# VectorE's order in the slots of an attention pipeline: statistics and division ahead of q, reciprocal behind v, output projection in the last block

## Chip, cores and metric

The kernel runs on one core of a Trainium2 chip. The metric is the device time of one execution in microseconds (us). The kernel before takes 1013.86 us, the median of three runs (1013.26 to 1014.37). All operands are float32.

## What is computed

Sixteen sequences of 256 tokens with 256 features go through three attentions and a feed-forward part. Each attention has 16 heads of 16 features.

```
layer 0 (cross):  q = rms(x) @ Wq ; k, v = rms(ctx) @ Wk, Wv
                  x = rms(x + softmax(q k' * scale) v @ Wo)
layer 1 (self):   h = ln(x) ; q, k, v from h ; rope(q, k) ; causal softmax
                  x = x + attention @ sa_wo
layer 2 (cross):  h = ln(x) ; q from h, k and v from ctx ; rope(q, k)
                  x = x + attention @ ca_wo
feed-forward:     x + gelu(ln(x) @ fc1) @ fc2
```

## The kernel before

There are 48 attentions, three for each sequence. `ORDER` (line 31) lists their layers in the order of work: "000001101102102...102112122222". The loop at line 698 has one slot for each of them. Slot i computes the scores and values of attention i in blocks, four for layers 0 and 2 and three for the causal layer 1, and between the blocks it does pieces of its neighbours. The order of all instructions is written out by hand[...].

A block n of slot i begins with `scores(n)` (lines 463 to 497): TensorE computes scores (L476), ScalarE takes the exponential (L487), and for the causal layer GpSimd cuts the upper triangle (L494). `values(n - 1)` follows: TensorE multiplies the block before with v (L515); the last values of attention i-1 are done in block 0 of slot i. When the values of a feature half are complete, ScalarE copies them out (L529). The sums of the softmax come with them as an extra row, and the SyncE queue carries them through DRAM into a compact tile `sums` (L530, L539), while eight transfers put the values into `oT` (L544).

The pieces for the neighbours are these. The names are methods of `Att`.

- `stats(i + 2)`: mean and variance, or mean squares, on VectorE (L246, L256, L257), then an inverse root on GpSimd (L238, L239).
- `norm(i + 2)`: VectorE applies it (`xn`, L263). `turn(i + 2)`: TensorE transposes `xn` (L274) and ScalarE copies it out as `hT` (L279). Layer 0 has neither, its input is loaded transposed.
- `q(i + 1)` and `k(i + 1)`: projections on TensorE (L294). For layers 1 and 2 ScalarE adds the bias (`a`, L402), VectorE rotates (L406 to L435) and writes `qm` (L428) or `kT` (L435). For layer 0 VectorE writes `qm` from PSUM (L421) and ScalarE copies k (L437).
- `v(i + 1)`: a projection (L307), taken out of PSUM into `va` by VectorE (L448 or L456).
- `invert(i - 1)`: VectorE's reciprocal of `sums` (L553, L554), a check sum on GpSimd (L555), and two transfers through DRAM into the tile `first` (L556, L560).
- `divide(i - 2)`: VectorE spreads `first` over the features (L566) and multiplies `oT` with it (L570).
- `project(i - 2)`: the output projection on TensorE (L307), and the residual on VectorE (L576 or L579). For layer 0 mean squares (L246) and an inverse root on GpSimd follow.
- `finish(i - 2)`: for layer 0 alone, VectorE's last scaling (L584).
- `send` and `receive` (i + 2): for layer 0 alone, a small transpose on VectorE (L368) and transfers that spread the inverse root of x as `rq`.

In slot i of the kernel before, block 0 has stats, q and divide; block 1 has k and norm; the block before the last has project and send; the last block has finish, v, turn, receive and invert. In a slot of layer 1 the block before the last is block 1.

Projections, transposes and output projections share a PSUM pool of three buffers (`psD`, line 158). `fold_bias` (L189) and `fold_v` (L219, L226) fold biases into weights once, in block 0 of slot 2; `fold_gain` (L230) scales the weights in slots 2 to 4. After slot 47 comes a short passage with the last output projections, and then the feed-forward part for eight pairs of sequences (L622, L636, L641, L651, L660).

Of the kernel before, what the change touches and what calls it, by code (L numbers as in the profile page):

```python
# [46 lines left out]
def xattn_kernel(  # L47
# [56 lines left out]
    def load(b):  # L104
        load_x(b)
        load_y(b)

    def load_w(t, aps, eng):
        at = 0
        for a in aps:  # L110
            m = a.shape[1]
            eng.dma_start(out=t[:, :, at : at + m], in_=a.rearrange("(k p) n -> p k n", p=P))
            at += m
# [65 lines left out]
    def fold_bias():  # L179

        ps = dense_ps()
        sets = (
            [(sa_sb, 0, V_B1), (sa_sb, D, V_B1), (ca_sb, 0, V_B2), (ca_sb, 0, V_B2)],
            [(fc1_sb, j * D, V_B3) for j in range(4)],
        )
        for n, items in enumerate(sets):
            for k in range(KC):
                for j, (w, at, vcol) in enumerate(items):
                    nc.tensor.matmul(  # L189
                        ps[32 * j : 32 * j + 32, n * D : (n + 1) * D],  # L190
                        lhsT=vec[:, vcol + k : vcol + k + 1].to_broadcast([P, 32]),
                        rhs=w[:, k, at : at + D],
                        start=(k == 0), stop=(k == KC - 1), skip_group_check=True,
                    )
        sb = work.tile([P, 2 * D], F32, tag="a", name="fold")
        nc.scalar.copy(sb, ps)
        hop = dram.tile([4, 2 * D], F32, tag="fold", name="fold_hop", bufs=1)
        nc.sync.dma_start(out=hop, in_=sb[0:P:32])
        cols = ctile([P, 4, 2, KC], "cols")
        nc.sync.dma_start(  # L200
            out=cols.rearrange("p j n t -> p (j n t)"),
            in_=hop.rearrange("j (m p) -> p (j m)", p=P),
        )
        return cols

    def fold_cols(cols):
        qk = vec[:, V_QK : V_QK + 8].rearrange("p (n t) -> p n t", t=KC)
        nc.vector.tensor_tensor(qk_bias[:, 0:3], cols[:, 0:3, 0], qk[:, 0:3], ALU.add)
        nc.vector.tensor_copy(qk_bias[:, 3], qk[:, 3])
        nc.vector.tensor_tensor(  # L210
            fb1.rearrange("p (j t) -> p j t", t=KC), cols[:, :, 1],
            vec[:, V_FC1B : V_FC1B + FF // P].rearrange("p (j t) -> p j t", t=KC), ALU.add,
        )

    def fold_v():
        ps = dense_ps()
        for k in range(KC):
            for j in range(0, P, 32):
                nc.tensor.matmul(  # L219
                    ps[j : j + 32, :D],  # L220
                    lhsT=vec[:, V_B1 + k : V_B1 + k + 1].to_broadcast([P, 32]),
                    rhs=sa_sb[:, k, 2 * D : 3 * D],
                    start=(k == 0), stop=(k == KC - 1), skip_group_check=True,
                )
        row = bias_sb[:, R_SAV : R_SAV + D]
        nc.vector.tensor_tensor(row, ps[:, :D], row, ALU.add)  # L226

    def fold_gain(w, cols, vcol):
        for k in range(KC):
            nc.vector.tensor_scalar(  # L230
                w[:, k, cols], w[:, k, cols], vec[:, vcol + k : vcol + k + 1], None, ALU.mult
            )
# [358 lines left out]
    def att(i):  # L591
        if 0 <= i < N_ATT:
            return atts.setdefault(i, Att(i))
        return None

    def do(i, *names):
        a = att(i)
        for name in names:
            if a is not None:
                getattr(a, name)()  # L600
# [73 lines left out]
    def check(good, ones):  # L674
        ps = dense_ps()
        nc.tensor.matmul(ps[:1, :1], lhsT=good, rhs=ones, start=True, stop=True)
        nc.vector.tensor_copy(rows_good, ps[:1, :1])
# [3 lines left out]
    with tc.manual_schedule():  # L681
        do(0, "stats_x")
        fold_gain(w0_sb, slice(0, D), V_GQ)
        fold_gain(w0_sb, slice(D, 2 * D), V_GC)
        do(0, "turn", "spread", "q", "k", "stats_y")
        fold_gain(w0_sb, slice(2 * D, 3 * D), V_GC)
        nc.vector.tensor_copy(mask01, mask_u8)
        for va in vas:
            nc.gpsimd.memset(va[:, :, :, HD:], 1.0)
        do(1, "stats", "turn")  # L690
        load(3)
        load_w(sa_sb, sa, nc.sync)

        kept = {}
        for j in range(N_ATT):
            slot = next(i for i in range(max(j - 1, 0), N_ATT + 1) if (ORDER + [0])[i] != 1)
            kept.setdefault(slot, []).append(j)
        for i in range(N_ATT):
            a, last = att(i), att(i - 1)
            ahead = att(i + 3)  # L700
            if i > 1 and ahead is not None and ahead.layer == 0:
                load(ahead.b)
            for n in range(len(a.blocks)):
                a.scores(n)
                if n > 0:
                    a.values(n - 1)
                elif last is not None:
                    last.values(-1)
                final = len(a.blocks) - 1
                if n == 0:  # L710
                    if i == 0:
                        a.v()
                        do(1, "spread")
                    do(i + 2, "stats")
                    do(i + 1, "q")
                    do(i - 2, "divide")
                elif n == 1:
                    do(i + 1, "k")
                    do(i + 2, "norm")
                    for j in kept.get(i, ()):  # L720
                        att(j).keep()
                if n == final - 1:
                    do(i - 2, "project")
                    do(i + 2, "send")
                if n == final:
                    do(i - 2, "finish")
                    do(i + 1, "v")
                    do(i + 2, "turn", "receive")
                    do(i - 1, "invert")
                if i == 0 and n == 0:  # L730
                    load(4)
                    nc.sync.dma_start(out=bias_sb, in_=rows.partition_broadcast(P))
                    nc.sync.dma_start(out=turn_sb, in_=turn)
                if i == 0 and n == 1:
                    load_w(ca_sb, ca, nc.sync)
                if i == 0 and n == 2:
                    load_w(fc1_sb, [fc1], nc.sync)
                if i == 1 and n == 0:
                    load_w(sao_sb, [sa_o], nc.sync)
                    load_w(cao_sb, [ca_o], nc.sync)  # L740
                if i == 1 and n == 2:
                    load_w(fc2_sb, [fc2], nc.sync)
                    nc.sync.dma_start(
                        out=rope_sb, in_=rope.rearrange("(c p) t d -> p c t d", p=P)
                    )
                if i == 2 and n == 0:
                    cols = fold_bias()
                    fold_v()
                if i == 2 and n == 3:
                    fold_gain(sa_sb, slice(0, 3 * D), V_G1)  # L750
                if i == 3 and n == 3:
                    fold_cols(cols)
                    fold_gain(ca_sb, slice(0, D), V_G2)
                if i == 4 and n == 3:
                    fold_gain(fc1_sb, slice(0, FF), V_G3)
                if i == N_ATT - 2 and n == 1:
                    mlps[0].norm()
                if i == N_ATT - 1 and n == 2:
                    mlps[0].turn()
                if i == N_ATT - 1 and n == 3:  # L760
                    mlps[1].norm()

        last = att(N_ATT - 1)
        last.values(-1)
        do(N_ATT - 2, "divide")
        mlps[0].up(0)
        mlps[0].up(1)
        do(N_ATT - 2, "project")
        last.invert()
        mlps[0].up(2)  # L770
        mlps[1].turn()
        mlps[0].up(3)
        last.divide()
        last.project()
        for g in range(B // 2):
            if g > 0:
                for n in range(4):
                    mlps[g].up(n)
            if 0 < g and g + 1 < B // 2:
                mlps[g + 1].norm()  # L780
                mlps[g + 1].turn()
            mlps[g].down(0)
            mlps[g].down(1)
            if g == 1:
                found = count()
            if g == 2:
                check(*found)
# [411 lines left out]
```

## Time and profile before

The profile's span is 1012.3 us. Busy times by engine:

| engine | busy us | share of the span |
|---|---|---|
| TensorE (matmul) | 969.3 | 96% |
| VectorE | 555.8 | 55% |
| ScalarE | 535.9 | 53% |
| GpSimd | 276.0 | 27% |

The slots run from 10.9 us to about 775.6 us, where the feed-forward part starts. In the stretch from 800 to 1012 us VectorE is busy for 38.06 of 212 us; between 200 and 600 us it is busy for 68 to 70 us of each 100.

How to read it: TensorE is busy nearly all the time, so the places where it idles say what the other engines cost. A high average share of another engine says little, since it is the order of work within a slot that decides whether TensorE finds its input ready. In a timeline a line has its start, the time that it took, the engine, the line of the code, the operation, output and input, the count, and in brackets the engine's idle time ahead of it with what ended that.

### The profile page before, as it was taken

What the parts mean: (1) busy time and instruction counts of PE and PEld (TensorE: products, weight loads), DVE (VectorE), ACT (ScalarE), POOL (GpSimd) and SP (SyncE); (2) the same over time, 40 slices, a digit from 0 to 9 for tenths busy, and PEclk for the clock granted to TensorE, in tenths of its full rate; (3) what the DMA queues carried; (4) which work ended last, traced back from release to release, by engine and by line L of the source; (5) the groups of instructions that cost most, each with busy time, mean ns of one, the idle gap of its engine ahead of it and who ended that gap; (6) DMA issues with size and microseconds to landing.
All of it is one profiled execution on the core that took longest, in us unless ns stands there. A gap on an engine that the chain in (4) does not pass through costs nothing.

```text
span 1012.3 us, 28536 instructions
## 1 busy us (share of the span) xinstructions
PE 969.3 (96%) x11798; PEld 509.5 (50%) x11798; DVE 555.8 (55%) x1300; ACT 535.9 (53%) x709; POOL 276.0 (27%) x494
## 2 busy tenths in 40 slices
PE   8999899999999999999999998898998999999997
PEld 3444444454444444454544444444443766666765
DVE  4358676767766667767767667766664112222200
ACT  4567375666666576766666665465665122221221
POOL 3213544241433333241423332332213011111100
PEclk9999999999999999999999999999999999999999
DMA  9512121221212121211212111010001000000000
GB/s 320 165 33 63 26 63 28 69 61 34 65 29 67 30 63 30 69 45 46 67 29 69 26 24 26 15 23 21 20 22 27 12 21 15 17 22 21 22 22 24
DMA packets 65826, 46.86 MB, mean 46 GB/s; under 512 B 25364, under 2 KB 64788, under 8 KB 65688
## 3 DMA queue, kind: packets, MB, share of 16 engines
q1 hardware_dynamic: 64456, 43.89, 16.0%
q8 instruction: 95, 1.56, 0.7%
q10 hardware_dynamic: 1232, 1.07, 0.3%
q14 instruction: 43, 0.35, 0.1%
HBM read 26.54 MB, written 5.79 MB: 32 GB/s over the span
## 4 chain that ended last, share of the span: by engine, by line
PE 67%; DVE 15%; DMA 9%; SPq 3%; POOL 2%; issue 2%; ACT 1%; DVEq 0%; ACTq 0%; POOLq 0%
PE d L307 16%; PE S L476 11%; PE S L651 11%; PE d L636 11%; PE A L515 9%; PE d L294 8%; DMA hop<-sums 3%; DVE oT L570 3%; DVE inv L566 3%; DMA sums<-hop 2%; DMA yT<-in_yt 2%; SPq L544 2%; DVE qm L428 2%; DMA oT<-av 1%; PE d L274 1%
## 5 line engine op out<-in xcount | busy, mean ns | idle before, releaser
L487 ACT ACTIVATE pt<-S 128x1024 f32<-128x1024 f32 x224 | 217.4, 1022 | 151.5 <-PE S L476 151.3
L476 PE MATMUL S<-qm,kT 32*128 32x512 f32 (+1 forms) x1536 | 205.0, 603 | 1.3 <-ACT kT L437 0.7
L515 PE MATMUL A<-pt,va 128*32 128x256 f32 (+1 forms) x3072 | 189.2, 367 | 1.4 <-DVE sums L554 1.0
L487 ACT ACTIVATE pt<-S,sy 128x1024 f32<-128x1024 f32 x128 | 135.7, 1112 | 52.0 <-PE S L476 50.5
L515 PEld LDWEIGHTS A<-pt,va 128*32 128x32 f32 x3072 | 80.1, 109 | 156.4 <-issue 88.9
L641 ACT ACTIVATE gT<-d,fb 128x512 f32<-128x512 f32 x64 | 43.9, 687 | 164.3 <-PE d L636 164.3
L651 PE MATMUL S<-fc,gT 128*128 128x256 f32 x512 | 111.9, 380 | 0.0
L636 PE MATMUL d<-hT,fc 128*128 128x512 f32 x256 | 111.9, 594 | 0.0
L555 POOL TENSOR_TENSOR seen<-seen,sums 128x64 f32<-128x64 f32 x48 | 16.5, 344 | 345.5 <-DVE sums L554 343.0
L494 POOL TENSOR_SCALAR_AFFINE_SELECT pt<-pt 128x512 f32<-128x512 f32 x128 | 91.3, 731 | 57.0 <-ACT pt L487 57.0
L651 PEld LDWEIGHTS S<-fc,gT 128*128 128x128 f32 x512 | 97.0, 191 | 13.4 <-issue 0.9
L660 DVE TENSOR_TENSOR res<-S,cur 128x512 f32<-128x512 f32 (+1 forms) x17 | 11.1, 660 | 160.0 <-PE S L651 160.0
L476 PEld LDWEIGHTS S<-qm,kT 32*128 32x128 f32 x1536 | 62.9, 185 | 69.1 <-issue 34.3
L636 PEld LDWEIGHTS d<-hT,fc 128*128 128x128 f32 x256 | 48.4, 190 | 57.6 <-issue 56.5
L402 ACT ACTIVATE a<-d,qk_bias 128x256 f32<-128x256 f32 x128 | 53.7, 470 | 34.9 <-PE d L294 30.2
L283 POOL TENSOR_TENSOR cur<-cur,bias 128x512 f32<-128x512 f32 x48 | 60.8, 1271 | 4.4 <-DVE xn L263 4.4
L294 PE MATMUL d<-hT,sa 128*32 128x256 f32 x1024 | 61.1, 379 | 0.0
L263 DVE TENSOR_SCALAR xn<-cur,bmv,r_ln 128x256 f32<-128x256 f32 x96 | 48.6, 547 | 18.1 <-POOL r_ln L239 18.1
L238 POOL TENSOR_SCALAR r_ln<-bmv 128x2 f32<-128x2 f32 x48 | 10.5, 218 | 175.2 <-DVE bmv L257 174.3
L529 ACT COPY av<-A 128x512 f32<-128x512 f32 x96 | 56.7, 591 | 1.2 <-PE A L515 1.2
L456 DVE TENSOR_TENSOR va<-d,bias 128x512 f32<-128x512 f32 x32 | 22.1, 690 | 59.7 <-PE d L307 59.7
L406 DVE LOAD_MASK_SELECT u<-a x64 | 0.9, 14 | 86.6 <-ACT a L402 86.6
(105 smaller groups left out, 1228.4 us busy)
## 6 DMA issues: line engine op xcount, KB each, us to landing
oT<-av SPq DMA_DIRECT2D x384, 32.0 KB
cur<-in_x SPq DMA_DIRECT2D x16, 256.0 KB
xT<-in_xt SPq DMA_DIRECT2D x16, 256.0 KB
yT<-in_yt SPq DMA_DIRECT2D x16, 256.0 KB
y<-in_y SPq DMA_DIRECT2D x16, 256.0 KB
out<-res SPq DMA_DIRECT2D x15, 256.0 KB
fc<-in_fc SPq DMA_DIRECT2D x2, 1024.0 KB
rq<-rq_hop SPq DMA_DIRECT2D x14, 128.0 KB
```

What stands on the lines that cost most here:

```text
L263: nc.vector.tensor_scalar(xn[:, c, :], src[:, c, :], mv[:, c, 0:1], r[:, c : c + 1], ALU.subtract, ALU.mult,)
L283: nc.gpsimd.tensor_tensor(t, t, bias_sb[:, row : row + D].unsqueeze(1).to_broadcast([P, NC, D]), ALU.add)
L294: nc.tensor.matmul(ps[j : j + 32, t * S : (t + 1) * S], lhsT=w[:, k, at + t * P + j : at + t * P + j + 32], rhs=src[:, k, :], start=(k == ...
L307: nc.tensor.matmul(ps[j : j + 32, c * D : (c + 1) * D], lhsT=src[:, k, c * P + j : c * P + j + 32], rhs=w[:, k, at : at + D], start=(k == ...
L402: nc.scalar.activation(a[:, t], ps[:, t], AF.Identity, bias=bias[:, t : t + 1])
L476: nc.tensor.matmul(ps[:, j, 2 * m * u : 2 * m * (u + 1)] .rearrange("p (i s) -> p i s", i=2), lhsT=self.kT[r, t, kc * P : (kc + 1) * P], r ...
L487: nc.scalar.activation(pt[:, :, :w], ps[:, :, :w], AF.Exp, scale=scale)
L494: nc.gpsimd.affine_select(out=diag, in_=diag, compare_op=ALU.is_ge, fill=0.0, base=0, pattern=[[0, 2], [0, 2], [1, P]], channel_multiplier=-1,
L515: nc.tensor.matmul(self.av[32 * r : 32 * r + 32, i, q0:S], lhsT=self.va[:, kc, 8 * t + 2 * r + i, :], rhs=pts[r // 2][:, r % 2, i * m : (i ...
L529: nc.scalar.copy(av, self.av)
L636: nc.tensor.matmul(ps, lhsT=fc1_sb[:, k, f * P : (f + 1) * P], rhs=self.hT[:, k].rearrange("p i s -> p (i s)"), start=(k == 0), stop=(k == ...
L651: nc.tensor.matmul(ps[:, c, :D], lhsT=self.gT[f // 2][:, f % 2, i, c * P : (c + 1) * P], rhs=fc2_sb[:, f, :], start=(f == 0), stop=(f == F ...
```

## The change

The change moves calls within a slot. It removes no work and adds none.

- `divide(i - 2)` goes ahead of `q(i + 1)` in block 0, behind `stats(i + 2)`.
- `finish`, until now in the last block for attention i-2, is done in block 0 of the slot after, ahead of `stats` there: `do(i - 3, "finish")`.
- `v(i + 1)` and, behind it, `invert(i - 1)` go from the last block into the block before the last.
- `project(i - 2)` goes from the block before the last into the last block.
- `fold_bias` and `fold_v` go from block 0 of slot 2 into block 3 of slot 1.

It is meant to give VectorE its work in the order in which other engines need it, and to give the output projection more time until its input must be ready.

```diff
                     if i == 0:
                         a.v()
                         do(1, "spread")
+                    do(i - 3, "finish")
                     do(i + 2, "stats")
+                    do(i - 2, "divide")
                     do(i + 1, "q")
-                    do(i - 2, "divide")
                 elif n == 1:
                     do(i + 1, "k")
                     do(i + 2, "norm")
                     for j in kept.get(i, ()):
                         att(j).keep()
                 if n == final - 1:
-                    do(i - 2, "project")
+                    do(i + 1, "v")
+                    do(i - 1, "invert")
                     do(i + 2, "send")
                 if n == final:
-                    do(i - 2, "finish")
-                    do(i + 1, "v")
+                    do(i - 2, "project")
                     do(i + 2, "turn", "receive")
-                    do(i - 1, "invert")
...
-                if i == 2 and n == 0:
+                if i == 1 and n == 3:
                     cols = fold_bias()
                     fold_v()
```

## The prediction

> **What bounds the kernel now.** I read the busy times first, then TensorE's waits, then the timeline of one slot with a long wait.
>
> ```profile
> PE 969.3 (96%) x11798; PEld 509.5 (50%) x11798; DVE 555.8 (55%) x1300; ACT 535.9 (53%) x709; POOL 276.0 (27%) x494
> ```
>
> TensorE (PE) sets the end; it idles for 1012.3 - 969.3 = 43.0 us. The view of waits for PE says on whom:
>
> ```profile
> PE d L307 <- DVE oT L570: 31.8, 37, 3.9
> PE A L515 <- DVE sums L554: 1.0, 1, 1.0
> PE S L476 <- ACT pt L487: 0.6, 3, 0.3
> ```
>
> Three quarters of it is the output projection waiting for the divided `oT`: 37 waits, the longest 3.9 us. The timeline of slot 39 (layer 1), first PE, then VectorE (DVE):
>
> ```profile
> 625.64 1.91 PE L294 MATMUL d<-hT,sa 128*32 128x256 f32 x32
> 631.21 3.22 PE L307 MATMUL d<-w0o,oT 128*32 128x256 f32 x32 [3.66 <-DVE oT L570]
> ```
>
> ```profile
> 624.70 0.74 DVE L406 STREAM_SHUFFLE u<-a 128x512 f32<-128x512 f32 x1
> ...
> 628.27 1.51 DVE L428 TENSOR_SCALAR qm<-a,vec 128x512 f32<-128x512 f32 x2
> 629.72 0.01 DVE L566 LOAD_MASK_SELECT inv<-first  x1
> 629.72 0.71 DVE L566 STREAM_SHUFFLE inv<-first 128x512 f32<-128x512 f32 x1
> 630.46 0.69 DVE L570 TENSOR_TENSOR oT<-oT,inv 128x512 f32<-128x512 f32 x1
> 631.08 0.01 DVE L406 LOAD_MASK_SELECT u<-a  x1
> ```
>
> The division costs 1.4 us and waits for nothing itself. It comes late because q's rotation stands ahead of it in VectorE's queue, 5.02 us from 624.70 to 629.72, and VectorE had idled 3.07 us before that for ScalarE's `a`. The projection behind the wait took 3.22 us instead of 1.91. The table by windows shows why:
>
> ```profile
> 104.00:124.00 20.00, 18.64 (x288) 9.47 (x292) 13.27 (x33) 7.92 (x10) 7.99 (x14) 0.91 0.10 22
> 204.00:224.00 20.00, 20.00 (x324) 10.29 (x320) 12.05 (x30) 12.10 (x16) 10.47 (x19) 1.00 0.12 28
> ```
>
> The last columns are granted clock, DMA share and GB/s. After the 3.91 us wait at 104 us the clock is 0.91 over 20 us: 9% of 20 is 1.8 us lost. The waits of 3.66, 3.70 and 3.66 us (slots 39, 40, 42) are followed by such a loss too; the one of 3.25 us (slot 8) isn't.
>
> [...] L426 takes 1.00 us and the L428 pair 1.51 us in slot 39, where GpSimd cuts triangles, but 0.69 and 0.88 us in slot 13.
>
> **Part by part.** Steps on PE, start to start in the timeline: scores 1.07, values 0.89 (causal: 0.46, or 1.33 for the last), a projection 1.84, transposes 0.59 us. On VectorE: division 1.4, q rotated 3.6 (5.0 beside triangles), k 2.7, norm 0.65, v 0.6, reciprocal 0.35 to 0.55, layer 0's residual with mean squares 1.6, 1.1 until GpSimd's root, finish 0.9 to 1.6, statistics 1.2 (layer 0: 2.0, to 2.6 contended). From the end of a reciprocal until `first` has come I find 3.6 us at best (785.59 to 789.18) and 6.3 at worst (112.36 to 118.62); I take 4, and 6.3 where `rq` travels behind it.
>
> *Project later, divide earlier.* In slot 39 the projection would start v + scores + values = 1.84 + 1.07 + 0.46 = 3.37 us later, and the division is 5.0 us earlier: 8.4 us against a longest wait of 3.9. I expect this wait to go everywhere.
>
> *Plain slots, 10 to 37.* Read start to start of a slot's first scores, they take 430.78 us (172.87 to 603.65): layer 0 mostly 16.65, layer 2 15.65, layer 1 13.29, three of them 14.69, 14.10 and 14.69. Even a wait shown as 0.24 us costs 0.42 (613.63 is 0.42 past 612.32 + 0.89). Without it: 10 x 16.23 + 9 x 15.23 + 9 x 13.29 = 419.0, a gain of **11.8**. Is a new wait added? Behind the divide, which now waits for `first`, stand q, k, norm, v and reciprocal; PE waits for norm at turn, and for k a slot later. For a layer 0 slot, from its start: residual and root until 2.3, finish 3.9, statistics 5.1, divide 6.6 (`first` in by 1.4 to 4), q 10.2, k 13.0, norm 13.7. Turn needs it at 15.6: hidden, 1.9 us to spare. A layer 2 slot has no turn, and k is done at 11, slot end 15.2. In a layer 1 slot q is 1.4 and k is ScalarE's: spare. Finish, statistics, v and reciprocal therefore cost nothing.
>
> *Crowded slots.* Where a three-block slot rotates q and k (5, 8, 39, 40, 42), VectorE has 12.4 to 18.2 us of work for some 13 us of PE. Chaining the durations above:
> - Slots 5 to 9 take 80.3 us now (92.56 to 172.87). Without any wait 69.5. But the statistics (2.6), divide and q of slot 5 put kT at 15.0 us, and slot 6 wants it at 12.8: 2.2 wait. I get 71.9, saving 8.4.
> - Slots 38 to 42 take 89.25 (603.65 to 692.90), 72.8 without waits. Finish, statistics, divide, q, k and norm of slot 40 end 2.4 us after turn wants them; slots 39 and 42 miss by 0.4 each. With smaller slips 76.35, saving 12.9.
> - GpSimd's check sum now waits for the late reciprocal with the last triangles queued behind it, and the values of the next slot wait for these: 0.5 (39), 0.5 (40), 0.2 (42), 1.2 (5), 0.8 (8). `rq` comes late for slot 6: 1.0. Together -4.2.
> Net **17.1**. None of these waits reaches 3.25 us, so no half clock.
>
> *Start.* In slot 1 blocks 2 and 3 have no PE work between them, so scores wait for ScalarE: values start at 40.02 instead of 38.59. Now v stands in block 2 and the fold (2.7 us, moved as it is) in block 3: **1.45**. Its weights were loaded by 32 us, when DMA falls to 20 GB/s, and it would run near 42: no wait. *Slots 4 and 43 to 46*: 0.42 each, **2.1**. *Passage after slot 47*: the 2.31 us wait goes (three steps later), the reciprocal for the next one comes a little late: **2.2**.
>
> Sum 11.8 + 17.1 + 1.45 + 2.1 + 2.2 = 34.7, so 1013.86 - 34.7 = **979**.
>
> **Rivals.**
> *A, everything is gained.* If VectorE's slips in the crowded slots stay hidden, slots 5 to 9 take 69.5 and 38 to 42 72.8: 1013.86 - (10.8 + 16.5 + 11.8 + 1.45 + 2.1 + 2.8) = 968. For it: VectorE idles 3 us for `a` before most rotations now, which the divide fills. Against it: its 18.2 us of work in slot 5.
> *B, the wait only changes place in the crowded slots.* Turn, scores or triangles wait as long as the projection did, with the half clock: the 17.1 is lost, 996. For it: VectorE busy for 14.9 and 14.0 us in slots 39 and 40. Against it: until now the idle 3 us lay ahead of q.
> *C, slower.* The divide's wait for `first` now holds back q, k and norm in every slot. If `first` comes over 3 us after VectorE, the 28 plain slots lose some 1.5 us each at turn: 979 + 42 = 1021. For it: VectorE waited 16.6 us in 10 waits for `first`, and some trips took 6 us. Against it: the reciprocal comes a block earlier, so by the chain above even 6.3 us is covered in a layer 0 slot.
>
> **How the numbers follow.** Forecast 0.62, A 0.12, B 0.2, C 0.06. Between forecast and B all mixtures are possible, since the landing of `first` (3.6 to 6.3) and the contended rotation (3.6 to 5.0) move the crowded slots by 2 us each, ten slots by 10 to 14. So I put the range from 970, short of A, to 993, short of B. Slower is C less a little: 0.04; same 0.02; faster 0.94.
>
> **What would show it.** PE's wait for `oT` near zero instead of 31.8 us; slots of 16.2, 15.2 and 13.3 us in the middle; the clock at 1.00 after 100 us; new PE waits for kT in slot 6 and for `xn` at turn of slots 39, 40, 42, and on GpSimd's triangles, 8 to 10 us in all. Wrong would be: VectorE waiting long for `first` with PE waiting behind it in plain slots (C), or half clock still in slots 39 to 42 (B).

## The result, and the profile after

The kernel after takes 977.68 us, the median of four runs (977.05 to 978.01); the kernel before took 1013.67 us beside it. The ratio is 0.9644, with an interval of 0.9627 to 0.966. The forecast was 979 us in a range of 970 to 993. The profile's span falls by 37.1 us, from 1012.3 to 975.2.

The busy times on the page of the kernel after:

```profile
PE 959.1 (98%) x11798; PEld 512.1 (53%) x11798; DVE 555.9 (57%) x1300; ACT 536.4 (55%) x709; POOL 278.7 (29%) x494
```

VectorE and ScalarE did the same work. TensorE idles for 975.2 - 959.1 = 16.1 us instead of 43.0, and it is busy for 10.2 us less with the same 11798 matmuls. Most of those 10.2 us is the clock: in the slots of the kernel before lie four stretches of half clock (granted clock 0.50; the first from 104.81 to 108.22 us), each 3.41 us long and so worth 1.7 us, and in those of the kernel after none (1.00 from 10 to 740 us).

The waits of TensorE in the kernel after (for whom, then us in total, times, the longest):

```profile
PE S L476 <- DVE kT L435: 2.5, 1, 2.5
...
PE d L307 <- ACT gT L641: 1.7, 1, 1.7
PE d L274 <- DVE xn L263: 1.6, 1, 1.6
...
PE d L274 <- ACT av L529: 0.5, 2, 0.3
```

No wait stands under `oT` any more. (The one under `gT` ends with `oT` all the same; the last experiment comes back to it.) What has taken the place of the 37 waits is few and short. TensorE's timeline shows where (start, us, line, operation, count, and in brackets the idle time ahead of it): at the start of slot 6, in slots 39 and 42 (39 is shown), at the end of slot 40 and in the passage after slot 47.

```profile
102.51 1.93 PE L307 MATMUL d<-w0o,oT 128*32 128x256 f32 x32
106.91 1.14 PE L476 MATMUL S<-qm,kT 32*128 32x512 f32 x8 [2.46 <-DVE kT L435]
...
610.64 1.93 PE L307 MATMUL d<-w0o,oT 128*32 128x256 f32 x32
612.82 0.67 PE L274 MATMUL d<-ident,xn 128*128 128x128 f32 x4 [0.25 <-ACT av L529]
...
629.04 0.67 PE L274 MATMUL d<-ident,xn 128*128 128x128 f32 x4 [1.61 <-DVE xn L263]
...
745.82 1.93 PE L307 MATMUL d<-cao,oT 128*32 128x256 f32 x32 [1.65 <-ACT gT L641]
```

The output projection of slot 39, which had waited 3.66 us and then run for 3.22, starts at once and takes 1.93. VectorE's timeline of the same slot shows the new order:

```profile
600.99 0.75 DVE L566 STREAM_SHUFFLE inv<-first 128x512 f32<-128x512 f32 x1
601.77 0.69 DVE L570 TENSOR_TENSOR oT<-oT,inv 128x512 f32<-128x512 f32 x1
604.56 0.01 DVE L406 LOAD_MASK_SELECT u<-a  x1 [2.10 <-ACT a L402]
...
612.27 0.73 DVE L263 TENSOR_SCALAR xn<-cur,bmv,r_ln 128x256 f32<-128x256 f32 x2
```

The division is done at 602.46, 8.2 us before the projection asks for it, and the idle time for ScalarE's `a`, 3.07 us before, is 2.10. The last line is where the price is paid: `xn` comes at the very end, and the transposes wait for it.

The table by windows, in the first of the two stretches that the prediction showed (the last three columns are granted clock, DMA share and GB/s):

```profile
104.00:124.00 20.00, 17.12 (x275) 8.88 (x268) 15.06 (x36) 9.04 (x12) 10.31 (x20) 1.00 0.12 27
```

In this run the clock stays at 1.00 there, although TensorE still idles for 2.9 of the 20 us after 104 us.

Read in the timeline from the first scores of one slot to those of another, the 37.1 us lie here:

| stretch | before, us | after, us | gain | predicted |
|---|---|---|---|---|
| to the start of slot 5 | 92.56 | 91.17 | 1.4 | 1.9 |
| slots 5 to 9 | 80.31 | 74.17 | 6.1 | 5.4 |
| slots 10 to 37 | 430.78 | 418.62 | 12.2 | 11.8 |
| slots 38 to 42 | 89.25 | 76.13 | 13.1 | 11.7 |
| slots 43 to 46 | 64.80 | 63.52 | 1.3 | 1.7 |
| slot 47 to the end | 254.6 | 251.6 | 3.0 | 2.2 |

The last column sums the prediction's own terms: slots 5 to 9 are 8.4 less 1.2, 0.8 and 1.0, slots 38 to 42 are 12.9 less 0.5, 0.5 and 0.2, and slot 4 stands with the start.

### The profile page after: what moved, and what is told of

The parts are those of the page before. It is cut to its first block, busy times and chain, and to the rows that moved or that the text cites. A ratio compares the mean times of both kernels' runs of the same rounds, so it can differ in the third digit from the quotient of the medians.

```text
span 975.2 us, 28507 instructions
## 1 busy us (share of the span) xinstructions
PE 959.1 (98%) x11798; PEld 512.1 (53%) x11798; DVE 555.9 (57%) x1300; ACT 536.4 (55%) x709; POOL 278.7 (29%) x494
## 3 DMA queue, kind: packets, MB, share of 16 engines
q10 hardware_dynamic: 1232, 1.07, 0.3%
## 4 chain that ended last, share of the span: by engine, by line
PE 91%; DVE 5%; POOL 1%; issue 1%; ACT 1%; SPq 1%; DMA 1%; DVEq 0%; POOLq 0%
PE S L476 18%; PE A L515 17%; PE d L294 16%; PE d L307 15%; PE S L651 11%; PE d L636 11%; PE d L274 2%; PE d L622 1%; DVE u L410 1%; DVE u L406 1%; DVE a L410 1%; DVE sq L246 1%; SPq L544 0%; DVE qm L428 0%; DVE cur L584 0%
## 5 line engine op out<-in xcount | busy, mean ns | idle before, releaser
L476 PE MATMUL S<-qm,kT 32*128 32x512 f32 (+1 forms) x1536 | 202.8, 600 | 3.6 <-DVE kT L435 2.5
L515 PE MATMUL A<-pt,va 128*32 128x256 f32 (+1 forms) x3072 | 192.3, 367 | 0.8 <-POOL pt L494 0.3
L494 POOL TENSOR_SCALAR_AFFINE_SELECT pt<-pt 128x512 f32<-128x512 f32 x128 | 87.8, 701 | 79.9 <-ACT pt L487 79.7
L555 POOL TENSOR_TENSOR seen<-seen,sums 128x64 f32<-128x64 f32 x48 | 15.4, 321 | 268.3 <-DVE sums L554 176.4
L283 POOL TENSOR_TENSOR cur<-cur,bias 128x512 f32<-128x512 f32 x48 | 64.6, 1350 | 4.4 <-DVE xn L263 4.4
L579 DVE TENSOR_TENSOR cur<-d,cur 128x512 f32<-128x512 f32 x32 | 21.9, 683 | 60.9 <-PE d L307 60.9
L263 DVE TENSOR_SCALAR xn<-cur,bmv,r_ln 128x256 f32<-128x256 f32 x96 | 45.1, 511 | 18.1 <-POOL r_ln L239 18.1
L410 DVE TENSOR_TENSOR a<-a,turn 128x512 f32<-128x512 f32 x64 | 48.6, 759 | 2.2
```

Of the source, the lines that this page charges most:

```text
L283: nc.gpsimd.tensor_tensor(t, t, bias_sb[:, row : row + D].unsqueeze(1).to_broadcast([P, NC, D]), ALU.add)
L410: nc.vector.tensor_tensor(t, t, table.unsqueeze(1).to_broadcast([P, KC, S]), ALU.mult)
L476: nc.tensor.matmul(ps[:, j, 2 * m * u : 2 * m * (u + 1)] .rearrange("p (i s) -> p i s", i=2), lhsT=self.kT[r, t, kc * P : (kc + 1) * P], r ...
L494: nc.gpsimd.affine_select(out=diag, in_=diag, compare_op=ALU.is_ge, fill=0.0, base=0, pattern=[[0, 2], [0, 2], [1, P]], channel_multiplier=-1,
L515: nc.tensor.matmul(self.av[32 * r : 32 * r + 32, i, q0:S], lhsT=self.va[:, kc, 8 * t + 2 * r + i, :], rhs=pts[r // 2][:, r % 2, i * m : (i ...
```

## The experiments

The theory: VectorE takes its instructions in order (in slot 39 before, the division, which waited for nothing, began at 629.72 us, as q's last instruction ended), so the projection waited for a division that stood behind q. The change gives that consumer slack from both ends, and takes it from k, `norm` and `turn`. (The statistics stood ahead of q before as well; of the calls ahead of q, `finish` and the division are new.) The rivals: one end alone does all of it; or the division's new wait for `first` costs something; or the move of v matters in itself. `finish` was not moved by itself. All kernels below compute the whole of the reference. "Plain slots" are 10 to 37. The kernels ran on three chips, and each ratio is to the kernel before on the same chip: 1014.92 us for the first four experiments, 1013.71 for v and for the last one, 1014.41 for the other four. A difference of 1 or 2 us from the kernel after is therefore not read from the times but from the slots of the profiles, except in the last experiment, where both ran side by side.

**The earlier division alone**, on the kernel before:

```diff
                     do(i + 2, "stats")
+                    do(i - 2, "divide")
                     do(i + 1, "q")
-                    do(i - 2, "divide")
```

> The kernel before, with one thing changed: divide stands ahead of q in block 0; the output projection, v, invert and finish stay where they were. My theory: VectorE's order is one of two remedies that each cover most of the waits. The long waits for oT in slots 5, 8, 39, 40 and 42 and the half clock behind them go (first lands at about 624.2 us in slot 39, so oT is ready at 625.6, wanted at 627.5), and so do the 0.24 us waits in slots of layers 0 and 2. The waits of 1.2 us that end with first's landing (slots 6, 21, 33, 36) stay. New waits at turn and for kT of some 6 us come in the crowded slots. 984 to 990 us, PE's wait for oT 4 to 8 us. Rival, the projection's later place is what counts: the waits for oT only shift and over 1003 us remain.

Measured: 992.55 us (990.53 to 994.86), ratio 0.9784 (0.9751 to 0.9818), a miss. The plain slots take 420.75 us, so 10.0 of their 12.2 us are there. What is missing is elsewhere. TensorE's waits:

```profile
PE d L307 <- DVE oT L570: 6.3, 4, 2.6
PE d L274 <- DVE xn L263: 5.1, 3, 2.5
PE S L476 <- DVE kT L435: 2.6, 2, 2.1
```

Four waits for `oT` remain: in slot 9 (1.81 us), in the plain slots 21 and 36 (0.64 and 1.20) and in the passage (2.60). At each of them VectorE had waited 4.3 to 5.3 us for `first` ahead of the division. The new waits are there too, that for `xn` longer than in the kernel after. Slot 6 takes 18.24 us instead of 15.15 before: TensorE runs there at half clock for 6.83 us, worth 3.4 us, which I had not expected. The profiled run took 990.53 us at a granted clock of 0.995, so without that half clock it would, as an estimate, lie within the 984 to 990 that I expected.

**The later projection alone**, on the kernel before, with what it needs (v a block earlier, `finish` in the next slot); division and reciprocal stay where they were:

```diff
+                    do(i - 3, "finish")
                     do(i + 2, "stats")
...
-                    do(i - 2, "project")
+                    do(i + 1, "v")
                     do(i + 2, "send")
...
-                    do(i - 2, "finish")
-                    do(i + 1, "v")
+                    do(i - 2, "project")
```

> The kernel before, with the output projection in the last block, v in the block before the last, and finish in the next slot's block 0, as in the change; but divide stays behind q, and invert at the end of the last block. My theory: 3.4 to 3.8 us more time until oT is wanted covers all plain waits and nearly all of 3.9 us in the crowded slots; VectorE's work until kT and xn is the same in sum. 979 to 984 us. PE's wait for oT under 5 us, of which up to 2.3 in the passage after slot 47. Rival, the place of the divide is what counts: over 990 us.

Measured: 985.06 us (981.82 to 987.28), ratio 0.9692 (0.966 to 0.9724). All plain slots take 16.22, 15.19 and 13.3 us, as in the kernel after. So either end alone frees the plain slots, but for two of them (21 and 36) with the division. What is missing lies mostly in slots 39 to 43: 15.68, 17.74, 17.85, 15.68 and 17.84 us, against 13.68, 16.22, 16.77, 13.68 and 16.77 after. TensorE's timeline at the end of slot 39:

```profile
615.82 0.67 PE L274 MATMUL d<-ident,xn 128*128 128x128 f32 x4 [1.80 <-DVE xn L263]
...
617.61 2.79 PE L515 MATMUL A<-pt,va 128*32 128x128 f32 x32
```

The wait for `xn` is 1.80 us instead of 0.25, and the values behind it take 2.79 us instead of 1.51: half clock, after a wait of 1.80 us. It comes three times, 3.41 us each, 5.1 us lost in all. It does not come in every run: the profiled one took 987.28 us at a granted clock of 0.993, another 981.82 at 1.000.

**The division behind q again**, on the kernel after, to see what that part of the change adds once the projection is late:

```diff
-                    do(i - 2, "divide")
                     do(i + 1, "q")
+                    do(i - 2, "divide")
```

> The changed kernel, with divide put back behind q. My theory: with the projection late, oT is ready in time in all slots but slot 5, where PE waits some 1.5 us for it and then that much less for kT, since VectorE's sum of work ahead of kT is the same. No measurable change from the changed kernel: 977 to 979 us. Rival, divide ahead of q carries the gain: 985 us or more.

Measured: 983.78 us (982.63 to 985.29), ratio 0.9688 (0.9658 to 0.9719). My expectation of no change was wrong by about 5 us (4.5 by the two ratios). The plain slots are the same; slots 39 and 42 take 15.07 us each instead of 13.68, slot 8 13.74 instead of 12.71, and slot 47, up to the first matmul of the feed-forward part, 17.37 instead of 13.43. VectorE's waits for ScalarE's `a` tell why, in this kernel

```profile
DVE u L406 <- ACT a L402: 68.2, 30, 4.6
```

and in the kernel after, where the wait for `first` stands above it:

```profile
DVE inv L566 <- DMA first<-hop: 21.8, 14, 4.2
DVE u L406 <- ACT a L402: 21.4, 15, 2.6
```

VectorE has to wait for `a` in any case, since ScalarE makes it from TensorE's projection. A division of 1.4 us that stands ahead of q is done in that time and is free; behind q it pushes all that follows. In slot 39 `xn` starts 13.9 us after the slot's first scores instead of 12.5; of the 1.39 us that the slot loses, 0.95 is that longer wait and 0.30 a wait for `oT`. That matters only where VectorE has no slack, in the crowded slots. So the early division does two things: the projection gets its input earlier, and VectorE gets 1.4 us back. Slot 47 loses more, to half clock again; TensorE's timeline there:

```profile
729.46 2.04 PE L476 MATMUL S<-qm,kT 32*128 32x512 f32 x8 [0.17 <-ACT pt L487]
732.95 1.93 PE L515 MATMUL A<-pt,va 128*32 128x256 f32 x16 [1.44 <-POOL va L455]
734.81 2.09 PE L476 MATMUL S<-qm,kT 32*128 32x512 f32 x8
```

Around a wait of 1.44 us the half clock sets in: values of 1.07 us take 1.93 and scores of 1.14 take 2.09. The granted clock of this run is 0.996. The loss is not half clock alone: a run with a granted clock of 1.000 still took 982.83 us.

**The reciprocal at the end again**, on the kernel after. This asks whether the division's wait for `first` costs anything (rival C):

```diff
                     do(i + 1, "v")
-                    do(i - 1, "invert")
...
                     do(i + 2, "turn", "receive")
+                    do(i - 1, "invert")
```

> The changed kernel, with invert put back at the end of the last block, so the reciprocal comes a block later and divide, still ahead of q, finds first not yet landed. This tries the rival that was slower. My theory: VectorE's wait for first grows from 21.8 us to over 100; in plain slots the spare 1.9 us at turn hides most of it, in crowded slots 2 to 3 us each come through: 980 to 988 us. The rival's mechanism at full size (every slot loses 1.5 us or more at turn): over 1010 us.

Measured: 979.59 us (978.65 to 980.86), ratio 0.9653 (0.9625 to 0.9682). VectorE's wait for `first` grows fivefold:

```profile
DVE inv L566 <- DMA first<-hop: 106.2, 46, 5.4
```

The plain slots do not notice: 16.22, 15.19 and 13.3 us. VectorE's other waits shrink in turn, for v (L448) from 31.1 to 15.4 us and for the output projection (L579) from 60.9 to 47.5. In slots 39, 40 and 42 the transposes wait longer (6.1 us in all), but slots 6, 9, 41 and 43 are shorter by 1.28, 0.74, 0.55 and 0.55 us: GpSimd's check sum, which waits for the reciprocal, no longer holds up triangles queued behind it (in slot 41 of the kernel after it starts at 630.16 us, after 5.68 us of waiting, and the triangles at 630.43). By the two profiles the early reciprocal is worth 1.7 us, which the intervals of the two ratios do not separate from nothing. Rival C falls: with 106 us of waiting for `first` no plain slot loses.

**v in the last block again**, behind the output projection, on the kernel after:

```diff
-                    do(i + 1, "v")
                     do(i - 1, "invert")
                     do(i + 2, "send")
...
                     do(i - 2, "project")
+                    do(i + 1, "v")
```

> The changed kernel with v put back into the last block, behind the output projection; all else as changed. My theory: v's move is what makes the projection's move free, since each block needs one projection to cover ScalarE's exponentials. The block before the last of each four-block slot then has no PE work besides scores and values, and the scores after it wait some 1.4 us, as in slot 1 of the kernel before: 30 slots by 1.4 us, 1015 to 1023 us, no faster than before. Causal slots, whose block 1 still has k, keep their length. Rival, v's place is free: 977 to 980 us.

Measured: 1008.85 us (1008.5 to 1009.2), ratio 0.995 (0.9935 to 0.9966): nearly all is lost, though less than expected. A layer 0 slot takes 17.54 us instead of 16.22 and a layer 2 slot 16.33 instead of 15.19; the causal ones stay at 13.3. TensorE's list of waits

```profile
PE S L476 <- ACT pt L487: 6.9, 32, 0.3
```

shows only 6.9 us, but the scores after such a wait are stretched. TensorE's timeline of a plain slot:

```profile
224.76 1.07 PE L515 MATMUL A<-pt,va 128*32 128x256 f32 x16
226.09 2.13 PE L476 MATMUL S<-qm,kT 32*128 32x512 f32 x8 [0.26 <-ACT pt L487]
228.15 1.07 PE L515 MATMUL A<-pt,va 128*32 128x256 f32 x16
```

ScalarE's timeline beside it:

```profile
224.92 2.12 ACT L487 ACTIVATE pt<-S,sy 128x1024 f32<-128x1024 f32 x2 [0.26 <-PE S L476]
226.93 0.58 ACT L529 COPY av<-A 128x512 f32<-128x512 f32 x1
227.40 2.14 ACT L487 ACTIVATE pt<-S,sy 128x1024 f32<-128x1024 f32 x2
```

Scores and values of a block keep TensorE for 1.07 + 0.89 = 1.96 us, its exponentials keep ScalarE for 2.12 and the copy-out for 0.47 more. A projection beside them (1.84 us) hides that; a block with none lets TensorE run into ScalarE. So the move of v is what lets the projection move without leaving a block bare. Moving v alone was not tried; it would leave the last block bare instead.

**The fold in slot 2 again**, on the kernel after:

```diff
-                if i == 1 and n == 3:
+                if i == 2 and n == 0:
```

> The changed kernel, with the fold of the biases put back into block 0 of slot 2. My theory: its 2.7 us of PE work no longer fill the hole in block 3 of slot 1, where scores then wait for ScalarE's exponentials: 1.2 to 1.5 us slower than the changed kernel, about 979.0 us, and all of it in slots 1 and 2. Rival, the fold's place is free: 977.7.

Measured: 980.63 us (979.59 to 981.14), ratio 0.9657 (0.9639 to 0.9675). Slots 1 and 2 take 34.85 us instead of 32.24, 2.6 more. TensorE's timeline:

```profile
41.85 2.13 PE L476 MATMUL S<-qm,kT 32*128 32x512 f32 x8 [0.26 <-ACT pt L487]
...
52.45 1.93 PE L294 MATMUL d<-yT,w 128*32 128x256 f32 x32 [1.08 <-issue]
...
109.23 1.89 PE L476 MATMUL S<-qm,kT 32*128 32x512 f32 x8 [2.47 <-DVE kT L435]
```

The first line is a bare block again, with the stretched scores of the experiment before: its values start at 43.91, 1.44 us later than the steps ahead of them add up to (40.51 + 0.89 + 1.07). The second, 1.08 us, was not predicted. The two folds stand behind q there, and the three together take all buffers of `psD`; VectorE empties q's at 52.35, having waited 4.67 us for `rq`. By these times k waits for that buffer; I did not test it apart. The third line is slot 6, which the fold does not touch. Its wait for `kT` is that of the kernel after, 2.47 us for 2.46, but here half clock sets in at 109.49, and the scores take 1.89 us instead of 1.14. Slot 6 as a whole takes 15.45 us instead of 15.02.

**The check sum later**, on the kernel after, so that the triangles don't wait behind it:

```diff
-            nc.gpsimd.tensor_tensor(seen, seen, sums, ALU.add)
...
                     do(i + 2, "turn", "receive")
+                    do(i - 1, "tally")
```

> The changed kernel, with GpSimd's check sum (the addition to seen) taken out of invert and done at the end of the last block; the reciprocal stays where it is. My theory: the last triangles no longer stand behind an instruction that waits for a late reciprocal, so slots 6, 9, 40, 41 and 43 lose what they have over their sum of steps: 15.02 to 13.9, 14.48 to 13.7, 16.22 to 15.7, and 16.77 to 16.2 twice, 3.5 us in all, 974 us. Rival, the values there wait for the exponentials themselves: 977.7.

Measured: 978.23 us (977.53 to 980.35), ratio 0.9633 (0.9615 to 0.965): no gain, where I had expected one. Slots 9 and 43 do fall to 13.74 and 16.22 us. But TensorE's waits grow elsewhere:

```profile
PE d L274 <- DVE xn L263: 4.2, 3, 2.3
PE S L476 <- DVE kT L435: 2.8, 1, 2.8
```

The last triangles now run while VectorE rotates k and applies `norm`. In slot 39 the addition at the end of that rotation (L435) takes 1.00 us instead of 0.69, and the two instructions of `norm` together 1.04 instead of 0.73, so `xn` comes later: 0.94 us of waiting instead of 0.25. In slots 40 and 42 the wait grows likewise (2.29 us for 1.61, 0.94 for 0.30), and in slot 6 `kT` comes 0.3 us later. The prediction had read the like from the trace of before. The additions L426 and L435 read two tiles each, L428 and `norm` one, and both kinds take longer beside the triangles: in slot 39 before L426 takes 1.00 us and the L428 pair 1.51, in slot 13 0.69 and 0.88. And half clock returns twice in the profiled run (980.35 us); here it is in the windows, at slot 6:

```profile
100.00:120.00 20.00, 17.14 (x240) 8.80 (x232) 15.82 (x33) 7.48 (x10) 11.85 (x20) 0.83 0.12 29
```

The clock of 0.83 costs 0.17 x 20 = 3.4 us.

**`norm` ahead of k**, on the kernel after, so that the transposes find `xn`:

```diff
-                    do(i + 1, "k")
                     do(i + 2, "norm")
+                    do(i + 1, "k")
```

> The changed kernel, with norm ahead of k in block 1. My theory: VectorE is late by its whole sum of work, so the wait for xn at turn (1.61 us in slot 40, 0.25 and 0.30 in 39 and 42) becomes in part one for kT, 0.65 us later, at the next slot's scores: 1.0 to 1.2 us gained, 976.6 us. Rival, only norm's place is at fault: all 2.2 us gained, 975.5 us.

Measured: 977.65 us (976.89 to 978.92), ratio 0.9629 (0.9611 to 0.9648), no gain that can be told, where I had expected 1.0 to 1.2 us. The wait for `xn` is gone, and 1.39 us of waiting for `kT` stand at slot 41 instead: in slot 40 VectorE itself is the bound, and its order only chooses who waits. The 0.25 and 0.30 us in slots 39 and 42, which the profile of after puts down to `av`, go as well, so they were for `xn`. In sum slots 39 to 43 take what they took, 77.2 us for 77.1. Slot 5 has no `norm` (attention 7 is layer 0), so nothing changes ahead of slot 6. But there the 2.47 us wait for `kT` is again followed by half clock, at 108.02, and the slot takes 16.05 us instead of 15.02.

**The scaling of the fc1 weights later**, on the kernel after: 1.41 us of VectorE's work in slot 4 that nothing needs before slot 47.

```diff
-                if i == 4 and n == 3:
+                if i == 14 and n == 3:
```

> The changed kernel, with the scaling of fc1 (two VectorE instructions, 1.41 us together) done in slot 14 instead of at the end of slot 4. My theory: in slot 5 VectorE waits for GpSimd's root right behind it, so only 0.7 to 0.9 us of the 1.41 shorten the 2.46 us wait for kT at slot 6: 976.8 us. Rival, VectorE's sum counts in full: 1.4 us, 976.3 us. Both are little; the wait for kT in the profile decides, 1.6 to 1.8 or 1.05 us.

Measured: 976.45 us (976.22 to 977.6), ratio 0.962 (0.9602 to 0.9638). Slot 5 falls from 15.74 to 15.13 us. The time as a whole differs from the kernel after by less than the intervals tell. Of the 1.41 us only 0.6 arrive, part of the rest being VectorE's wait for GpSimd's root of the residual, 1.13 us instead of 0.60. The wait for `kT`, which I had meant to decide by, falls only to 2.30 us: TensorE itself comes there 0.44 us earlier, since the values behind the third scores of slot 5 no longer wait for triangles (0.65 us instead of 1.09). Here work is taken out of a stretch in which VectorE is the bound.

**Three of the kind together**, on the kernel after: that scaling later; the check sum late for attention 7 alone, whose delay slot 9 pays; and, in the passage, the second feed-forward pair's norm behind the last but one division. It stood ahead of that division in VectorE's queue, which is the 1.65 us wait at 745.82 (the profile names `gT`, but `oT` ends at 745.72).

```diff
-            nc.gpsimd.tensor_tensor(seen, seen, sums, ALU.add)
+            if self.i != 7:
+                self.tally()
...
+                    if i == 8:
+                        do(7, "tally")
...
-                if i == 4 and n == 3:
+                if i == 14 and n == 3:
...
-                if i == N_ATT - 1 and n == 3:
-                    mlps[1].norm()
...
+        mlps[1].norm()
```

> The changed kernel with three small moves where the runs until now show a wait and no new one: the scaling of fc1 in slot 14, GpSimd's check sum in the last block for slot 8 alone, and the statistics and norm of the second feed-forward pair behind the division in the passage after slot 47. My theory: 0.6 us in slot 5, 0.7 in slot 9, and the 1.65 us wait after slot 47, which ends with oT: 2.9 us together, 974.8 us where the changed kernel takes 977.7. Rival: a wait moved in a crowded slot brings the half clock or another wait and gives it back: 977 us or more.

Measured: 974.41 us (974.13 to 975.11), ratio 0.9612 (0.9598 to 0.9625). The kernel after took 977.16 us (976.78 to 978.1) beside it, ratio 0.9638 (0.9625 to 0.9651). So this version is faster than both kernels. Slot 9 falls from 14.50 to 13.74 us, and in TensorE's timeline the passage's projection follows at once:

```profile
735.50 7.13 PE L640 MATMUL d<-hT,fc 128*128 128x512 f32 x16
742.56 1.93 PE L307 MATMUL d<-cao,oT 128*32 128x256 f32 x32
```

## Why the prediction was right, and where it was not

**Plain slots, 11.8: measured 12.2.** Every slot is at the sum of its steps. That each end alone gives 10.0 us or all of it shows that the slack was ample, as "8.4 us against a longest wait of 3.9" had it.

**Crowded slots, 17.1: measured 19.2.** The kind of each wait was right, and most sizes: `kT` in slot 6 2.46 us for 2.2, `xn` in slot 40 1.61 for 2.4, in slots 39 and 42 0.25 and 0.30 for 0.4. The held-up triangles are the 1.28, 0.74, 0.55 and 0.55 us of slots 6, 9, 41 and 43, predicted as 1.2 (5), 0.8 (8), 0.5 (40) and 0.2 (42) by the slot ahead; the 0.5 of slot 39 did not come. Nor did the 1.0 us for a late `rq`: VectorE waits for `rq`, 25.9 us in ten waits, but no wait of TensorE follows. The terms that were too large, 1.0, 0.8 and 0.5, less the 0.3 by which the wait for `kT` was longer, are the 2 us by which the sum was low. Of new waits and held-up triangles 7.7 us came, where the prediction had said 8 to 10.

**Start, 1.45: the bare block that the fold put back leaves costs 1.44.** In the profile of the kernel after slot 4 begins only 0.93 us earlier, because the first scores came 0.6 us later than before, at 11.54; in the kernels here they lie anywhere from 10.92 to 11.60, with no relation to the change that I can see. Slot 4 gave 0.46 for 0.42. **Slots 43 to 46: 1.3 for 1.7**, with the 0.55 of triangles in slot 43 inside. **Passage, 2.2: measured 3.0**, in part by luck. Of the 2.31 us wait 1.65 is still there: the step overlooked that the second pair's norm stands ahead of the division. Other gains, which it had not counted, made up for that: the 0.97 us wait ahead of slot 47's second values fell to 0.20, and its last values no longer wait for exponentials (0.17 and 0.29).

**"None of these waits reaches 3.25 us, so no half clock": the profiled run has none in the slots, but by luck; the step does not hold.** It took the limit from the five long waits of before, four over 3.6 us with half clock and one of 3.25 without. Kernels close to this one fall to half clock at waits of 1.73, 1.80, 2.11, 2.29, 2.47 and 2.77 us. The 2.47 us is the very wait for `kT` in slot 6 that the kernel after has too: with the fold put back and with `norm` ahead of k half clock follows it, in the profiled run of the kernel after it does not. It may come in other runs of that kernel. The profiled one took 977.05 us at a granted clock of 0.999; two others took 978.0 at 0.997, and a loss of 0.002 x 976 = 2.0 us would be about one stretch of 3.41 us, which costs 1.7 (an estimate; there is no trace of these two). Rival B's half clock at turn is what the later projection alone did in slots 39 to 43, for 1.1 to 2.0 us each.

**The early division.** The part by part costed it by when `oT` is ready; that it fills VectorE's idle time stood only under rival A, "which the divide fills". The chain of durations still had it in the sum, since it put the division into the time before q. By the third experiment it is worth about 5 us, half clock included.

**Rival C** needed the wait for `first` to reach TensorE in the plain slots. It does not at 106 us of waiting, five times what the kernel after has.

## What to carry to other kernels

Where one engine waits for another that works in order, look at both ends: can the producer's instruction stand ahead of one that waits for a third engine, and can the consumer come later? The first also gives the producer its idle time back, which counts where the producer is short of time; the second must leave no stretch without the work that hid something else, here one projection per block beside the exponentials. Where the producer itself is the bound, a new order only moves the wait (to `kT` instead of `xn`); taking work out of the stretch is what shortens it.

## What was not expected of the hardware

The half clock does not follow from the length of one wait. It came after 1.73 us with the later projection alone. It did not come after the 2.46 us of slot 6 in the kernel after, nor after the 3.25 us of slot 8 before, where the clock stays at 1.00, nor with the reciprocal at the end, where the longest waits for `xn` and for `kT` are 2.8 us each and the profiled run has a granted clock of 1.000. After nearly the same wait in slot 6 it came with the fold put back (2.47 us) and not in the kernel after (2.46).

In the slots of the kernel before it lasted 3.41 us each time. Its starts there, 104.81, 630.46, 650.94 and 685.07 us, lie 525.65, 20.48 and 34.13 us apart, which is 154, 6 and 10 times 3.413 us. In the 3.41 us ahead of each start TensorE idled for 2.74, 2.91, 2.60 and 2.98 us. What sets these times no run here shows.

In slot 47 with the division behind q a wait of 1.44 us was enough. There the scores ahead of the wait ran two at a time, where otherwise four start together. TensorE's timeline from 729.47 to 729.9 us with the division behind q:

```profile
729.46 0.70 PE L476 MATMUL S<-qm,kT 32*128 32x512 f32 x2 [0.17 <-ACT pt L487]
```

And from 729.2 to 729.6 us in the kernel after:

```profile
729.16 0.71 PE L476 MATMUL S<-qm,kT 32*128 32x512 f32 x4
```

So a stretch in which TensorE counts as busy can hold fewer matmuls: eight scores take 2.04 us here and 1.14 there. That this counts together with a wait is a guess, and no run here varies the one without the other. The kernel after has scores stretched like these at 725.92 us (2.04 us), with 0.20 us of waiting behind them and no half clock.
